# The order of four matmuls in the 64-row slots of an attention-score loop

## The chip, the cores and the metric

The kernel runs on one core of a Trainium2 chip. The metric is device time in microseconds (us), the median of three runs. The engines are called PE (TensorE; PEld is its loading of weights), DVE (VectorE), ACT (ScalarE), POOL (GpSimd) and SP (which issues most DMAs).

## The reference, cut to what matters

Eight images of 128 channels and 36x36 pixels go through a convolutional attention block, then each image's 1296 pixels become tokens of 128 features, then an additive attention over the tokens, then a mixture of experts. The additive attention is where the time goes, and the change touches nothing else:

```
def _L1_attn_ref(x, mask, Wq, bq, Wk, bk, w, bw):
    q = jnp.einsum('bld,ed->ble', x, Wq) + bq
    k = jnp.einsum('bld,ed->ble', x, Wk) + bk
    t = jnp.tanh(q[:, :, None, :] + k[:, None, :, :])
    scores = jnp.einsum('bijd,d->bij', t, w) + bw[0]
    attn = jax.nn.softmax(scores, axis=-1)
    return jnp.einsum('bij,bjd->bid', attn, x)
```

Every pair of tokens i, j needs a sum of 128 weighted tanh values. The kernel doesn't take the tanh of each pair. It groups five or six features, and writes the sum of their weighted tanh as one fraction: the denominator is a product of (exponential of the query + exponential of the key) terms, multiplied out into 32 (for five features) or 64 (for six) products of a query factor and a key factor, and the numerator has the same products with other weights. So a group's denominator and numerator are matmuls with a contraction of 32 or 64 rows.

## The kernel before, in words

**Units and slots.** The score loop runs over 264 units: 8 images x 3 chunks of 432 queries x 11 tiles of keys. Ten tiles of a chunk have 128 keys, one (the remainder) has 16. A unit of 128 keys has 12 slots, `k` = 0 to 11, in four triples. In a triple the first two slots (`k % 3` = 0 and 1) hold groups of five features: two matmuls with contractions of 32 rows each. The third (`k % 3` = 2) is a **slot of six**: its two halves are rows 0 to 63 and rows 64 to 127, and each half has its own PSUM bank. There are 4 x 240 = 960 slots of six. A remainder unit has two slots of its own form, made at line 1159.

**A slot's work.** `denominators(p + LAG)`, with `LAG` = 3, issues the two denominator matmuls of the slot three places ahead into one `d` tile of two banks (there are two such tiles, so the tile is free when ACT has read the slot two places before), and then ACT's logarithm over both banks (line 1177). An exponential follows on ACT (line 1180): for `k % 3` = 0 at once, for the two slots that follow together, after the second one's logarithm. That gives `lq`, one over the denominator. Then `numerators(p)` issues the two numerator matmuls of this slot into two of four `n` banks; `terms(p, ns)` has DVE multiply each by `lq` (line 1211 for most slots, where the results `rp` are added up by POOL at line 1220; lines 1200 to 1207 for `k` = 1, 4, 7 and 10, where DVE adds them up itself). All other work that needs a PSUM bank (convolutions, projections, transposes: the matmuls at lines 279 and 283) takes its banks from the same four, in turn.

**What sets the order.** The program is emitted by hand, and each engine runs its own instructions in that order, with semaphores between engines. `matmul_turn` puts the other work's matmuls behind the slots of six (`TURNS` = 2, 5, 8, 11). So within a slot of six PE has, in order: denominator half 0 and half 1 of the slot three ahead, numerator half 0 and half 1 of this slot, then other work if any is due. They will be called d0, d1, n0 and n1. `products` issues them (line 1154); each is float32 and leaves two load-and-multiply passes in the trace, so a slot leaves four passes named `d` and four named `n`.

For a slot of six `p` the slot `p + 3` is a slot of six too, except for the last slot before each of the 24 remainder units and for the end of the loop: 935 of 960.

Of the kernel before, what the change touches and what calls it, by code (L numbers as in the profile page):

```python
# [9 lines left out]
F32 = mybir.dt.float32  # L10
# [9 lines left out]
CH = 432  # L20
# [6 lines left out]
NKT = len(KT)  # L27
# [20 lines left out]
SLOTS = []  # L48
# [7 lines left out]
LAG = 3  # L56
# [15 lines left out]
def kernel(  # L72
# [29 lines left out]
    mm = nc.tensor.matmul  # L102
# [27 lines left out]
    with ExitStack() as loop, ExitStack() as score:  # L130

        def pool(name, bufs, stack=loop, side="left", space=bass.MemoryType.SB):
            return stack.enter_context(
                tc.tile_pool(name=name, bufs=bufs, side=side, space=space)
            )
# [13 lines left out]
        ps_d = pool("ps_d", 2, score, "right", bass.MemoryType.PSUM)  # L149

        ps_n = pool("ps_n", 4, space=bass.MemoryType.PSUM)
# [19 lines left out]
        def load_raw_taps(w, name):  # L171
# [36 lines left out]
            out=gavg3, in_=gavg3, compare_op=ALU.is_ge, fill=0.0, base=0,  # L208
# [3 lines left out]
            out=gavg3, in_=gavg3, compare_op=ALU.is_ge, fill=0.0, base=C // G - 1,  # L212
# [191 lines left out]
        def conv_keys(b):  # L404
            k = convolved["k"] = big_tile("k0")
            if b == 0:
                taps["k"] = load_taps("wk_t")
            for r0, nr in KROWS:
                yield from conv_turns(
                    taps["k"], (r0, nr), 1, grid(k[:, r0 * WV : (r0 + nr) * WV], WV), True  # L410
                )
# [471 lines left out]
        def gating(b):  # L883
            yield from gate_logits(b, range(NCH))
            yield from gate_tokens(b)
# [184 lines left out]
        def early_shares():  # L1070

            t = one.tile(list(xpad.shape), F32, tag="xpad", name="shares0").rearrange(
                "p a b -> p (a b)"
            )[:, :N]
            nc.sync.dma_start(t, gpair[0])
            shares_of[0] = [t[:, c * CH : (c + 1) * CH] for c in range(NCH)]
            shares_of[1] = load_pieces(
                gpair[1],
                lambda: kstp.tile([128, NF // 2, 128], F32, tag="ks", name="shares1").rearrange(
                    "p q t -> p (q t)"  # L1080
                )[:, :CH],
            )

        def first_weights():

            t = one.tile(list(xwin.shape), F32, tag="xwin", name="w0").rearrange(
                "p j n -> p (j n)"
            )
            w1s[0] = t[:, : EG * HID].rearrange("p (e h) -> p e h", e=EG)
            nc.sync.dma_start(w1s[0], weight1[:EG, :128, :].rearrange("e d h -> d e h"))  # L1090
            b1_s = t[:E, EG * HID : (EG + 1) * HID]
            nc.sync.dma_start(b1_s, weight1[:, 128, :])
            b2_s = t[:, (EG + 1) * HID : (EG + 1) * HID + O]
            for h in range(2):
                nc.sync.dma_start(b2_s[E * h : E * (h + 1)], weight2[:, HID, :])
            ffn_bias.extend((b1_s, b2_s))

        def residuals(n):

            for b in range(n):  # L1100
                load_residual(b)
                yield step()
# [10 lines left out]
        units = [(b, c, j) for b in range(NB) for c in range(NCH) for j in order]  # L1113
        slots = []
        for u, (b, c, j) in enumerate(units):
            slots += [(u, k) for k in range(len(REM_SLOTS) if j == NKT - 1 else NP)]
        kf_of, qf_of, lq_of, live = {}, {}, {}, {}

        def banks(u, k):
            return 2 if units[u][2] < NKT - 1 else len(REM_SLOTS[k])  # L1120
# [10 lines left out]
        def prefetch(u):  # L1131
            if u < len(units) and u not in kf_of:
                b, c, j = units[u]
                assert (b, j) in made
                n = 128 if j < NKT - 1 else 32
                kf = kfp.tile([128, NF, 128], F32, tag="kf", name="kf")
                nc.sync.dma_start(
                    kf[:, :, :n], kd[b][j].rearrange("p (q t) -> p q t", t=128)[:, :, :n]
                )
                kf_of[u] = kf  # L1140

        def new_block(b, c, q):
            qf = qfp.tile([128, 2, CH], F32, tag="qf", name="qf")
            qf_of[b, c, q] = qf
            return query_block(b, c, q, qf)

        def products(u, k, part, outs):

            b, c, j = units[u]
            kf = kf_of[u]  # L1150
            if j < NKT - 1:
                q, rows = SLOTS[k]
                for h in range(2):
                    mm(outs[h][:, :CH], kf[rows[h], q, :], qf_of[b, c, q][rows[h], part, :],  # L1154
                       start=True, stop=True)
                return
            for out, bank in zip(outs, REM_SLOTS[k]):
                for i, (q, rows) in enumerate(bank):
                    mm(out[32 * i : 32 * i + 32, :CH], kf[rows, q, :32],  # L1159
                       qf_of[b, c, q][rows, part, :], start=True, stop=True)  # L1160

        def denominators(p):

            if p >= len(slots):
                return
            u, k = slots[p]
            d = ps_d.tile([128, 2, 512], F32, tag="d", name="d")
            n = banks(u, k)
            products(u, k, 0, [d[:, h, :] for h in range(n)])
            g, o = group_of[p]  # L1170
            if g == p:
                alone = p in ends
                lq_of[g] = lp.tile(
                    [128, 2 if alone else 4, CH], F32, tag="lq1" if alone else "lq", name="lq"
                )
            lq = lq_of[g]
            nc.scalar.activation(lq[:, o : o + n, :], d[:, :n, :CH], AF.Ln)  # L1177
            if p in ends:
                some = lq[:, : o + n, :]
                nc.scalar.activation(some, some, AF.Exp, scale=-1.0)  # L1180

        def numerators(p):
            ns = [ps_n.tile([128, 512], F32, tag="n", name="n") for _ in range(banks(*slots[p]))]
            products(*slots[p], 1, ns)
            return [ps[:, :CH] for ps in ns]

# [37 lines left out]
        def sums(u):  # L1224

            s = live.pop("p")
            ending(u).tensor_add(s[:, 0, :], s[:, 0, :], s[:, 1, :])  # L1227
            d = live.pop("d")
            ending(u).tensor_add(d, s[:, 0, :], d)  # L1229
            return d  # L1230
# [49 lines left out]
        def take_turns(p, k):  # L1280
            for lane in lanes:
                if lane.due(p, False) and (k not in DVE_PAIRS or lane is first_of_all):
                    lane.run(p)
# [53 lines left out]
        for p in range(LAG):  # L1337
            denominators(p)
# [5 lines left out]
        for p, (u, k) in enumerate(slots):  # L1344
            b, c, j = units[u]
            rem = j == NKT - 1
            if k == 0:
                prefetch(u + 2)
                if c == 0 and j == 1:
                    if b > 0:  # L1350
                        gates.append(gating(b - 1))
                    if b == NB - 1:
                        gates.append(residuals(4))
                        first_weights()
                        early_shares()
                    if b + 1 < NB:
                        background.extend(
                            (normal(b + 1), conv_keys(b + 1), layer0(b + 1), tokens(b + 1),
                             keys(b + 1, range(NKT)))
                        )  # L1360
            take_turns(p, k)
            denominators(p + LAG)
            ns = numerators(p)
            terms(p, ns)
            if pending and pending[0][0] <= p:
                exps(p, *pending.popleft()[1:])
            last = p + 1 == len(slots) or slots[p + 1][0] != u

            if j == order[-1] and u + 1 < len(units):
                for q in NEXT_AT.get(k, ()):  # L1370
                    first_of_all.append(new_block(*units[u + 1][:2], q))
            elif j == order[-2] and last and u + 2 < len(units):
                first_of_all.append(new_block(*units[u + 2][:2], IN_TURN[0]))
            behind_rem = k == 0 and u > 0 and units[u - 1][2] == NKT - 1
            matmul_turn(
                p, k == 1 if rem else k in TURNS or behind_rem,
                lanes[:1] if behind_rem else lanes,
            )
            if last and rem:
                first_of_all.append(rem_scores(p, u, live.pop("rem")))  # L1380
            elif last:
                pending.append((p + 7, u, sums(u)))
# [74 lines left out]
    hidden, hidden_t, outs = {}, {}, deque()  # L1457
# [154 lines left out]
```

## Time and profile before

| | |
|---|---|
| median of 3 runs | 6008.39 us (6008.08 to 6008.49) |
| the profiled execution | 6001.25 us, of which the span of the trace is 5999.3 us |
| granted TensorE clock | 0.996 of full speed |
| score loop, 260 to 5880 us of the span: PE busy | 5304 of 5620 us |
| the same: ACT busy | 5189 us |
| the same: DVE busy | 4575 us |
| the same: POOL busy | 4396 us |
| denominators' and numerators' passes (line 1154) | 11,520 each, median 522 ns |

Matmul passes overlap: a pass of 432 columns is listed with 522 ns, but passes on the same rows begin 361 ns apart, and passes on different rows run beside each other. So PE's busy share says little by itself; the times at which passes begin say more.

### The profile page before, as it was taken

The page shows a single profiled execution, that of the slowest core. Times are in us where ns is not written, and L with a number is a line of the kernel's source. Part 1 is how long each engine was busy: PE and PEld are TensorE (multiplying, and loading weights), DVE is VectorE, ACT ScalarE, POOL GpSimd, SP SyncE. Part 2 cuts the span into 40 slices and gives each one's busy share as a digit, 9 for nine tenths or more (in the row PEclk, how much of TensorE's full clock was granted, in tenths as well). Part 3 has the DMA queues.
Part 4 walks back from the last instruction along what each step waited for, and adds up shares of the span by engine and source line. Part 5 has one row for each costly group of instructions (what it writes and reads, how often), then busy time and mean ns, then how long its engine had stood idle before and what let it go on. Part 6 is the DMA issues. An engine that isn't in the chain of part 4 may idle for free.

```text
span 5999.3 us, 94469 instructions
## 1 busy us (share of the span) xinstructions
PE 5629.9 (94%) x33507; PEld 2937.7 (49%) x33507; DVE 4780.5 (80%) x9566; ACT 5359.6 (89%) x5995; POOL 4581.9 (76%) x2870
## 2 busy tenths in 40 slices
PE   8999999999999999999999999999999999998888
PEld 5554455545554454544545445454445544544334
DVE  4787878878788788877888778887878878788884
ACT  3999999999989899889998989989998999999993
POOL 5777777877778868778788777877777777778872
PEclk9999999999999999999999999999999999999999
DMA  1200021001110011100111001110011100210007
GB/s 60 70 23 23 29 73 40 21 25 41 62 39 21 27 54 48 38 24 23 64 38 40 23 23 67 38 36 23 25 66 37 36 23 25 77 57 22 30 26 284
DMA packets 151705, 270.43 MB, mean 45 GB/s; under 512 B 45568, under 2 KB 77568, under 8 KB 151232
## 3 DMA queue, kind: packets, MB, share of 16 engines
q1 hardware_dynamic: 151008, 263.84, 13.0%
q8 instruction: 264, 4.33, 0.3%
q14 instruction: 209, 1.71, 0.1%
q10 hardware_dynamic: 224, 0.55, 0.0%
HBM read 200.15 MB, written 63.93 MB: 44 GB/s over the span
## 4 chain that ended last, share of the span: by engine, by line
PE 58%; DVE 23%; ACT 9%; issue 7%; POOL 2%; DMA 1%; DVEq 0%; POOLq 0%; ACTq 0%
PE d L1154 19%; PE n L1154 12%; DVE rp L1211 9%; PE pa L279 7%; DVE n L1205 7%; ACT lq L1177 6%; PE pc L279 5%; DVE accd L1207 4%; PE s L279 3%; PE pk L279 3%; PE pq L279 2%; PE n L1159 1%; PE d L1159 1%; POOL accp L1220 1%; ACT lq L1180 1%
## 5 line engine op out<-in xcount | busy, mean ns | idle before, releaser
L1220 POOL TENSOR_TENSOR accp<-accp,rp 128x864 f32<-128x864 f32 x1439 | 2911.2, 2023 | 962.1 <-DVE rp L1211 933.8
L1154 PE MATMUL n<-qf,kf 32*128 32x432 f32 (+1 forms) x11520 | 2996.2, 552 | 12.1 <-ACT qf L806 7.4
L1154 PE MATMUL d<-qf,kf 32*128 32x432 f32 (+1 forms) x11520 | 2777.2, 558 | 206.5 <-ACT lq L1177 197.6
L1177 ACT ACTIVATE lq<-d 128x864 f32<-128x864 f32 x2928 | 2480.1, 876 | 338.7 <-PE n L1154 252.7
L1211 DVE TENSOR_TENSOR rp<-n,lq 128x432 f32<-128x432 f32 x3912 | 2180.1, 600 | 701.0 <-PE n L1154 570.4
L1180 ACT ACTIVATE lq<-lq 128x864 f32<-128x864 f32 (+1 forms) x1944 | 2495.9, 1284 | 61.6
L1154 PEld LDWEIGHTS d<-qf,kf 32*128 32x128 f32 (+1 forms) x11520 | 1029.1, 184 | 1359.6 <-ACT lq L1177 997.1
L1154 PEld LDWEIGHTS n<-qf,kf 32*128 32x128 f32 (+1 forms) x11520 | 1259.9, 185 | 667.0 <-issue 286.8
L1207 DVE TENSOR_TENSOR accd<-n,accd 128x432 f32<-128x432 f32 x1440 | 866.1, 601 | 24.6
L1205 DVE TENSOR_TENSOR n<-n,lq 128x432 f32<-128x432 f32 x1440 | 809.4, 607 | 47.2 <-PE n L1154 29.0
L1218 POOL TENSOR_TENSOR accp<-rp 128x864 f32<-128x864 f32 x240 | 485.2, 2022 | 250.8 <-DVE rp L1211 250.0
L1229 POOL TENSOR_TENSOR accd<-accp,accd 128x432 f32<-128x432 f32 x239 | 265.0, 1109 | 18.7
L279 PE MATMUL pa<-xh,e 128*108 128x129 f32 x1920 | 251.0, 280 | 30.0 <-DVE accd L1207 28.7
L279 PEld LDWEIGHTS pa<-xh,e 128*108 128x108 f32 x1920 | 220.2, 173 | 118.3 <-DVE accd L1207 97.4
L1227 POOL TENSOR_TENSOR accp<-accp 128x432 f32<-128x432 f32 x239 | 263.7, 1103 | 12.2
L807 POOL TENSOR_SCALAR qf<-qf,cs_s 128x432 f32<-128x432 f32 x192 | 260.1, 1364 | 4.1 <-ACT qf L806 4.0
L477 POOL TENSOR_TENSOR tot<-tot,e 116x432 f32<-116x432 f32 x192 | 211.7, 1103 | 16.6 <-ACT e L486 13.2
L279 PE MATMUL s<-q,k 128*116 128x432 f32 x480 | 209.6, 548 | 9.5 <-DVE accd L1207 7.5
L279 PE MATMUL pa<-e,vw 116*128 116x432 f32 x480 | 200.8, 541 | 0.0
L279 PEld LDWEIGHTS pk<-xT,a_k 128*128 128x128 f32 x1408 | 165.6, 193 | 57.9 <-DVE accd L1207 42.8
L486 ACT ACTIVATE e<-s 116x432 f32<-116x432 f32 x240 | 118.8, 521 | 83.5 <-PE s L279 80.8
L279 PE MATMUL pk<-xT,a_k 128*128 128x128 f32 (+1 forms) x1408 | 180.7, 281 | 2.4 <-DVE accd L1207 1.3
(260 smaller groups left out, 3754.6 us busy)
## 6 DMA issues: line engine op xcount, KB each, us to landing
kf<-kd SPq DMA_DIRECT2D x239, 512.0 KB
kd<-ks SPq DMA_DIRECT2D x158, 256.0 KB
w<-in_weight_dram SPq DMA_DIRECT2D x32, 1024.0 KB
wk_t<-wk_t_d SPq DMA_DIRECT2D x7, 768.0 KB
wv_t<-wv_t_d SPq DMA_DIRECT2D x7, 768.0 KB
wq_t<-wq_t_d SPq DMA_DIRECT2D x7, 768.0 KB
x<-in_x_dram SPq DMA_DIRECT2D x8, 648.0 KB
t<-tokd SPq DMA_DIRECT2D x96, 54.0 KB
```

What stands on the lines that cost most here:

```text
L279: mm(out, lhsT, rhs, **kw)
L807: nc.gpsimd.tensor_scalar(qf[:, 1, :], qf[:, 0, :], feat["cs_s"][:, q : q + 1], None, ALU.mult)
L1154: mm(outs[h][:, :CH], kf[rows[h], q, :], qf_of[b, c, q][rows[h], part, :], start=True, stop=True)
L1177: nc.scalar.activation(lq[:, o : o + n, :], d[:, :n, :CH], AF.Ln)
L1180: nc.scalar.activation(some, some, AF.Exp, scale=-1.0)
L1205: mult(ns[h], ns[h], lq[:, o + h, :])
L1207: nc.vector.tensor_add(live["d"], ns[h], live["d"])
L1211: mult(rp[:, h, :], n, lq[:, o + h, :])
L1218: nc.gpsimd.tensor_add(live["p"], live["r"], rp)
L1220: ending(u if k == NP - 1 else 0).tensor_add(live["p"], live["p"], rp)
L1227: ending(u).tensor_add(s[:, 0, :], s[:, 0, :], s[:, 1, :])
L1229: ending(u).tensor_add(d, s[:, 0, :], d)
```

## The change

Where both slot `p` and slot `p + 3` are slots of six, the four matmuls are issued in the order n0, d1, d0, n1 in place of d0, d1, n0, n1. ACT's logarithm (and, where it is due, exponential) is emitted behind all four. The tiles, the number of instructions, their operands and their engines stay as they are; everywhere else the order stays too.

```diff
+        def is_six(p):
+            return p < len(slots) and units[slots[p][0]][2] < NKT - 1 and slots[p][1] % 3 == 2
...
+        def sixes(p):
+
+            outs = n_banks(p), d_banks(p + LAG)
+            for at, part, h in ((p, 1, 0), (p + LAG, 0, 1), (p + LAG, 0, 0), (p, 1, 1)):
+                u, k = slots[at]
+                q, rows = SLOTS[k]
+                out = outs[0][h] if part else outs[1][:, h, :]
+                mm(out[:, :CH], kf_of[u][rows[h], q, :], qf_of[(*units[u][:2], q)][rows[h], part, :],
+                   start=True, stop=True)
+            reciprocals(p + LAG, outs[1])
+            return [ps[:, :CH] for ps in outs[0]]
...
-            denominators(p + LAG)
-            ns = numerators(p)
+            if is_six(p) and is_six(p + LAG):
+                ns = sixes(p)
+            else:
+                denominators(p + LAG)
+                ns = numerators(p)
```

`d_banks` and `n_banks` allocate the tiles as `denominators` and `numerators` did, and `reciprocals(p, d)` is the second half of the old `denominators`: the logarithm and the exponential on ACT, unchanged.

More of the change, by code (lines that the diff above doesn't have):

```diff
@@ L1160, in products, with d_banks, n_banks @@
                        qf_of[b, c, q][rows, part, :], start=True, stop=True)
+        def is_six(p):
+            return p < len(slots) and units[slots[p][0]][2] < NKT - 1 and slots[p][1] % 3 == 2
+        def d_banks(p):
+            return ps_d.tile([128, 2, 512], F32, tag="d", name="d")
+        def n_banks(p):
+            return [ps_n.tile([128, 512], F32, tag="n", name="n") for _ in range(banks(*slots[p]))]
+        def sixes(p):
[8 more added lines that the diff above has]
+            return [ps[:, :CH] for ps in outs[0]]
         def denominators(p):
@@ L1165, in denominators, with reciprocals @@
                 return
[L1166 to L1169, printed above, removed]
+            d = d_banks(p)
+            products(*slots[p], 0, [d[:, h, :] for h in range(banks(*slots[p]))])
+            reciprocals(p, d)
+        def reciprocals(p, d):
+            n = banks(*slots[p])
             g, o = group_of[p]
@@ L1182, in numerators @@
         def numerators(p):
-            ns = [ps_n.tile([128, 512], F32, tag="n", name="n") for _ in range(banks(*slots[p]))]
+            ns = n_banks(p)
             products(*slots[p], 1, ns)
```

## The prediction

> **What bounds the kernel now.** I read the page's busy times first, then the list of waits, then the timeline around slots of six. The page (engine, busy us, share, instructions; then a group with its mean duration in ns and the idle time before it):
>
> ```profile
> PE 5629.9 (94%) x33507; PEld 2937.7 (49%) x33507; DVE 4780.5 (80%) x9566; ACT 5359.6 (89%) x5995; POOL 4581.9 (76%) x2870
> ...
> L1177 ACT ACTIVATE lq<-d 128x864 f32<-128x864 f32 x2928 | 2480.1, 876 | 338.7 <-PE n L1154 252.7
> ```
>
> Two engines share the bound: PE and ACT. Who waits for whom (us in total, times, longest):
>
> ```profile
> PEld d L1154 <- ACT lq L1177: 997.1, 1244, 2.7
> ...
> DVE rp L1211 <- PE n L1154: 570.4, 661, 10.5
> ...
> ACT lq L1177 <- PE n L1154: 252.7, 312, 2.9
> ...
> PE d L1154 <- ACT lq L1177: 197.6, 395, 2.0
> ```
>
> PE waits for ACT to free a d tile (197.6 us of true idleness), and ACT waits for PE's denominators (252.7 us, put down to the n passes that end beside them). Neither has much to spare. The timeline shows a stretch without other work (start, duration, engine, operation, count, idle before):
>
> ```profile
> 3000.13 0.87 ACT L1177 ACTIVATE lq<-d 128x864 f32<-128x864 f32 x1
> ...
> 3001.06 0.99 PE L1154 MATMUL d<-qf,kf 64*128 64x432 f32 x4 [0.84 <-ACT lq L1177]
> ...
> 3001.86 1.66 ACT L1177 ACTIVATE lq<-d 128x864 f32<-128x864 f32 x2
> 3001.89 0.89 PE L1154 MATMUL n<-qf,kf 64*128 64x432 f32 x4
> ...
> 3002.79 0.63 PE L1154 MATMUL d<-qf,kf 32*128 32x432 f32 x2
> ...
> 3002.88 1.12 DVE L1211 TENSOR_TENSOR rp<-n,lq 128x432 f32<-128x432 f32 x2 [0.85 <-PE n L1154]
> ```
>
> Here ACT bounds: the logarithm ends at 3001.00, d0 and d1 begin at 3001.06 after 0.84 us of idle PE. n0 and n1 begin 0.83 us later, the next slot 0.90 us after that. d is complete at 2.05 (that is, 3002.05); the second logarithm of the "x2", the one that reads it, begins at 1.86 + 1.66 - 0.89 = 2.63. So it has 0.58 us to spare. And a stretch with other work:
>
> ```profile
> 5290.47 0.99 PE L1154 MATMUL d<-qf,kf 64*128 64x432 f32 x4
> ...
> 5291.05 1.65 ACT L1177 ACTIVATE lq<-d 128x864 f32<-128x864 f32 x2
> ...
> 5291.30 0.89 PE L1154 MATMUL n<-qf,kf 64*128 64x432 f32 x4
> ...
> 5292.73 1.64 ACT L1180 ACTIVATE lq<-lq 128x1728 f32<-128x1728 f32 x1
> ...
> 5294.28 0.87 ACT L1177 ACTIVATE lq<-d 128x864 f32<-128x864 f32 x1
> ...
> 5295.21 0.99 PE L1154 MATMUL d<-qf,kf 64*128 64x432 f32 x4 [0.24 <-ACT lq L1177]
> ```
>
> Here PE came to the slot late: no idle time before d. ACT's logarithms, exponential and next logarithm follow without a gap, and the next slot of six waits for the last of them.
>
> I measured all 935 slots from the trace's single passes in this way. In **463 PE came late** (no idle before d beyond the 0.09 us of changing from 32 to 64 rows); in the other 472 it had waited, 225.6 us in all.
>
> **The change, part by part.** Nothing is removed: four matmuls on two row halves before, four after.
>
> *PE's own time.* Before, d0 beside d1, then n0 beside n1: 0.83 + 0.90 us. After, where nothing waits, n0 beside d1, then d0 beside n1: the same. Where PE waits for ACT, n0 now runs in the wait; but rows 64 to 127 still have d1 and then n1 to do from the logarithm's end, the same 1.7 us, and the next slot, of 32 rows, begins only when n1 has ended (2.79 against 1.89 + 0.89 = 2.78 above). So the filled wait is worth **0**.
>
> *The logarithm, where PE came late (463).* d0 is now in the second pair, so d is complete where n was: 0.83 + 0.89 = 1.72 after the slot's start, against 0.99, some 0.72 us later. The spare time of the logarithm there is 0.43 us in the mean (median 0.41). Late logarithms, slot by slot, max(0, 0.72 + wait for n0 - spare): 167 us in 381 slots. In the 5290 stretch: d complete at 1.46 becomes 2.18, the logarithm moves from 1.81 to 2.2, nearly 0.4 us. What ACT then loses it can regain in its own later gaps before the next slot of six. At 2414.02 the first logarithm of a triple begins after 0.25 us of idleness, which would swallow most of it; at 5294.28 there is none. Subtracting those gaps slot by slot leaves 87 us. The rest is swallowed where the next slot's d tile had been free for a while when PE arrived; subtracting that too leaves **42 us**. At 5295.21 PE was waiting already, so there the whole 0.3 to 0.4 us count.
>
> *The logarithm, where PE had waited (472).* n0 begins in the wait, so d0 is held back by 0.43 us in the mean, and the logarithm can spare 0.54 or more: 17 us late, 6 after ACT's gaps, **1 us** at the end.
>
> *The wait of n0.* n0's bank is freed by DVE's product of the slot two before. At the old place of n0 it was free in nearly all slots. At the new place, 0.83 us earlier, it isn't in 83 of the 463, by 15 us together. Behind it in PE's queue stand d1 and d0, for whose bank ACT is long done. Does a waiting n0 hold them up? The row: in the stretch above an n pass on other rows begins at 3003.62, ahead of d passes (3003.63) that were issued before it, so passes of different rows don't keep strict order once issued. The Trainium skill's "TensorE: Matmul & The Clock Gate", Part 3, under what overlaps and what doesn't, says that matmuls start and end strictly in program order, and only weight loads are pulled ahead. By a free order this costs 0, by the rule **15 us** on PE. The rule speaks against the change, and since the row's 0.01 us are of passes past their waits, I take the rule. In the waiting slots n0 is often some 0.1 us late, in front of an idle PE: 5 us at most, taken as **5**.
>
> *DVE.* It can multiply n0 up to 0.7 us earlier, n1 as before; the second product then ends up to 0.55 us sooner, where DVE stood idle (0.85 us in the stretch above). Such waits before a six's first product, cut at 0.57 us each, sum to 72 us, but only 25 us of them lie in front of a next slot to which PE comes late; before the others ACT is what PE waits for. In most slots to which PE comes late DVE has a backlog and doesn't wait for n0. Ends: 0 and -25; I take **-8**, since few of these products are the ones that PE waits for.
>
> POOL's sum needs both products; it has 76% of the span and its waits are not on PE's path: 0. No DMA moves. In the end: 42 + 1 + 15 + 5 - 8 = **+55 us**. Against the profiled execution's 6001.25 that is 6056; the median of the runs stands 7.1 us above it, so 6063.
>
> **The rivals.**
> 1. *ACT's slack is worth less than I count.* A late logarithm uses up gaps that an earlier one counted already, and the leeway of the next slot goes too. Without the leeway of the next slot's d tile: 87 + 6 + 20 = +113, that is 6121; with nothing absorbed at all, 167 + 17 + 20 = +204, that is 6212, an extreme. For it: ACT has 92% of the loop. Against it: its 430 us of gaps lie mostly before the first logarithm of a triple, just behind the six.
> 2. *DVE is the loop's true pace-maker*, and n0 in front pays: the chain of waits has DVE at 23%, through products of n. If all 72 us came through and a late logarithm were absorbed (it needs a mean absorption of 0.36 us in 381 slots), the time would be 6008 - 72 + 20 = 5956; with the 25 us that lie before late slots and nothing else, 5983. It decides once the earlier second product brings more than the 55 + 8 us of cost, about 0.07 us in each of 935 slots. Against it: DVE waited for n before only some 250 of them.
> 3. *No difference*: ACT's gaps swallow all of the delay, and PE's lateness at n0 is recovered while it would have waited for DVE in the next slots of five: within 12 us of 6008.
>
> That the order does not come out as written is unlikely: each engine keeps the emitted order.
>
> **How the numbers follow.** A kernel of 6008 us can be told from itself within about 0.2%, 12 us; that is what "same" means here. My forecast's case (+20 to +90): 0.52; rival 1: 0.24; rival 3: 0.12; rival 2: 0.12. Some of the forecast's case ends in "same": faster 0.12, same 0.12, slower 0.76. The likeliest case has 6028 to 6098 for itself. The range reaches up into rival 1 and down over rival 3, 6003 to 6130.
>
> **What would show it.** Right: the logarithm's idle time (338.7 us, 252.7 of it from PE) grows by over 50 us, and now in front of a six's logarithm too; in late slots the d passes of a six end 0.7 us later; PE's idle time before d doesn't fall in sum, and the passes of a slot of six still take 1.7 us where nothing waits; DVE's 570.4 us of waiting for n falls. Wrong: ACT's idle time unchanged or smaller, or slots of five (whose n passes now start up to 0.5 us late) becoming shorter by more than ACT loses.

## The result, and the profile after

| | before | changed |
|---|---|---|
| median | 6008.28 us (5 runs, 6006.62 to 6008.49) | 6059.85 us (5 runs, 6055.9 to 6061.79) |
| ratio, with 95% interval | | 1.0084 (1.0073 to 1.0096) |
| profiled execution, span | 6001.25, 5999.3 us | 6058.24, 6056.3 us |

The change costs 52 us. Forecast were 6063 us, in a range of 6003 to 6130. What was line 1177 before is line 1201 now, 1211 is 1235, and the four matmuls of the 935 reordered slots are line 1178. First the page of the changed kernel (busy us, share, instructions; then groups with busy us, mean ns, and the idle time before them):

```profile
PE 5797.1 (96%) x33507; PEld 3074.5 (51%) x33507; DVE 4774.7 (79%) x9566; ACT 5394.2 (89%) x5995; POOL 4584.9 (76%) x2870
...
L1201 ACT ACTIVATE lq<-d 128x864 f32<-128x864 f32 x2928 | 2521.8, 878 | 380.0 <-PE n L1154 202.8
L1235 DVE TENSOR_TENSOR rp<-n,lq 128x432 f32<-128x432 f32 x3912 | 2185.7, 599 | 712.9 <-PE n L1154 498.9
...
L1178 PE MATMUL d<-qf,kf 64*128 64x432 f32 x3740 | 1429.6, 553 | 45.4 <-ACT lq L1201 45.0
```

PE is busier by 167 us with the same 33,507 passes: a wait for ACT in which an n0 now runs is counted as busy. That is no gain. ACT has 34.6 us more of busy time and 22.4 us more of idle time (span less busy: 639.7 before, 662.1 now), together the 57.0 us by which the span grew. The idle time before its logarithms went from 338.7 to 380.0. The list of waits says where the new part is (us in total, times, longest):

```profile
PEld n L1178 <- DVE rp L1235: 592.8, 839, 1.8
...
ACT lq L1201 <- PE n L1154: 202.8, 264, 2.9
PEld d L1178 <- ACT lq L1201: 146.2, 170, 1.7
...
ACT lq L1201 <- PE n L1178: 97.2, 300, 1.4
```

The first line is idle time of the weight loads alone, with passes mostly still running beside it; PE itself stood idle before an n0 for want of DVE for 15.2 us by the page. The last line is new: 300 times ACT stood in front of a six's logarithm for a pass of line 1178 that ends the slot. It is put down to n1, which ends beside d0. Counted over the single logarithms of the two traces: the gaps before those of slots of six grew from 40.8 us (49 gaps) to 136.0 us (349), those before the first logarithm of a triple shrank from 262.4 to 211.5 us. This is the timeline of PE in a slot to which PE came late (start, duration, engine, operation, count):

```profile
3028.89 0.63 PE L1178 MATMUL n<-qf,kf 64*128 64x432 f32 x1
3028.90 0.63 PE L1178 MATMUL d<-qf,kf 64*128 64x432 f32 x1
3029.36 0.52 PE L1178 MATMUL n<-qf,kf 64*128 64x432 f32 x1
3029.37 0.88 PE L1178 MATMUL d<-qf,kf 64*128 64x432 f32 x2
3029.73 0.52 PE L1178 MATMUL n<-qf,kf 64*128 64x432 f32 x1
3030.09 0.52 PE L1178 MATMUL d<-qf,kf 64*128 64x432 f32 x1
3030.09 0.52 PE L1178 MATMUL n<-qf,kf 64*128 64x432 f32 x1
3030.54 0.63 PE L1154 MATMUL d<-qf,kf 32*128 32x432 f32 x2
```

n0 and d1 run beside each other, then d0 and n1. The last d pass ends at 3030.61, 1.72 us after the slot's start, where it was 0.99 before. ACT in the same stretch:

```profile
3029.57 0.87 ACT L1201 ACTIVATE lq<-d 128x864 f32<-128x864 f32 x1
3030.64 0.89 ACT L1201 ACTIVATE lq<-d 128x864 f32<-128x864 f32 x1 [0.21 <-PE n L1178]
3031.57 1.64 ACT L1204 ACTIVATE lq<-lq 128x1728 f32<-128x1728 f32 x1
3033.12 0.87 ACT L1201 ACTIVATE lq<-d 128x864 f32<-128x864 f32 x1
```

The logarithm begins 0.03 us after that pass has ended, with 0.21 us of idle time in front, and the exponential and the next logarithm follow late without a gap that could make up for it. The next slot of six pays:

```profile
3032.76 0.99 PE L1178 MATMUL n<-qf,kf 64*128 64x432 f32 x2
3034.04 0.99 PE L1178 MATMUL d<-qf,kf 64*128 64x432 f32 x4 [0.29 <-ACT lq L1201]
3034.87 0.88 PE L1178 MATMUL n<-qf,kf 64*128 64x432 f32 x2
3035.78 0.63 PE L1154 MATMUL d<-qf,kf 32*128 32x432 f32 x2
```

Here n0 runs in PE's wait for that logarithm, as the change has it. But d1 and n1 are still to come on rows 64 to 127, and the next slot begins 3035.78 - 3034.04 = 1.74 us after d; before it was 1.73 (3001.06 to 3002.79). The wait is filled and nothing is saved.

### The profile page after: what moved, and what is told of

Read it like the earlier page. It is cut to its first block, busy times and chain, and to the rows that moved or that the text cites. A ratio compares the mean times of both kernels' runs of the same rounds, so it can differ in the third digit from the quotient of the medians.

```text
span 6056.3 us, 94481 instructions
## 1 busy us (share of the span) xinstructions
PE 5797.1 (96%) x33507; PEld 3074.5 (51%) x33507; DVE 4774.7 (79%) x9566; ACT 5394.2 (89%) x5995; POOL 4584.9 (76%) x2870
## 4 chain that ended last, share of the span: by engine, by line
PE 63%; DVE 21%; ACT 7%; issue 7%; POOL 1%; DMA 1%; DVEq 0%; POOLq 0%; ACTq 0%
PE d L1154 14%; PE n L1154 9%; PE n L1178 8%; DVE rp L1235 8%; PE pa L279 7%; DVE n L1229 7%; PE d L1178 6%; PE pc L279 5%; ACT lq L1201 5%; DVE accd L1231 3%; PE s L279 3%; PE pk L279 3%; PE pq L279 2%; PE n L1159 1%; PE d L1159 1%
## 5 line engine op out<-in xcount | busy, mean ns | idle before, releaser
L1201 ACT ACTIVATE lq<-d 128x864 f32<-128x864 f32 x2928 | 2521.8, 878 | 380.0 <-PE n L1154 202.8
L1235 DVE TENSOR_TENSOR rp<-n,lq 128x432 f32<-128x432 f32 x3912 | 2185.7, 599 | 712.9 <-PE n L1154 498.9
L1154 PE MATMUL n<-qf,kf 32*128 32x432 f32 x7780 | 2121.8, 564 | 21.0 <-ACT qf L806 12.4
L1154 PE MATMUL d<-qf,kf 32*128 32x432 f32 (+1 forms) x7780 | 1832.3, 550 | 17.9 <-ACT lq L1201 15.6
L1178 PE MATMUL n<-qf,kf 64*128 64x432 f32 x3740 | 1685.3, 549 | 42.2 <-DVE rp L1235 15.2
L1178 PE MATMUL d<-qf,kf 64*128 64x432 f32 x3740 | 1429.6, 553 | 45.4 <-ACT lq L1201 45.0
L1154 PEld LDWEIGHTS n<-qf,kf 32*128 32x128 f32 x7780 | 851.3, 183 | 371.2 <-ACT qf L806 74.1
L1154 PEld LDWEIGHTS d<-qf,kf 32*128 32x128 f32 (+1 forms) x7780 | 732.1, 184 | 569.8 <-ACT lq L1201 263.1
L1178 PEld LDWEIGHTS n<-qf,kf 64*128 64x128 f32 x3740 | 624.2, 186 | 717.2 <-DVE rp L1235 592.8
L1178 PEld LDWEIGHTS d<-qf,kf 64*128 64x128 f32 x3740 | 562.6, 186 | 310.4 <-ACT lq L1201 146.2
L1251 POOL TENSOR_TENSOR accp<-accp 128x432 f32<-128x432 f32 x239 | 263.8, 1104 | 12.2
```

The costliest lines, as they stand in the source:

```text
L1178: mm(out[:, :CH], kf_of[u][rows[h], q, :], qf_of[(*units[u][:2], q)][rows[h], part, :], start=True, stop=True)
L1235: mult(rp[:, h, :], n, lq[:, o + h, :])
```

## The experiments

Two theories stood against each other. **L**: what costs is that d is complete 0.72 us later, so that ACT's logarithm is late. **W**: what costs is that n0, in front, may wait for its bank and holds d up.

**d1 in front.** No numerator stands ahead of d1 any more, and d is as late as in the change.

```diff
-            for at, part, h in ((p, 1, 0), (p + LAG, 0, 1), (p + LAG, 0, 0), (p, 1, 1)):
+            for at, part, h in ((p + LAG, 0, 1), (p, 1, 0), (p + LAG, 0, 0), (p, 1, 1)):
```

> Order d1, n0, d0, n1 in the same 935 slots: nothing stands in front of d any more, and d is still complete only with the second pair. Theory L (the cost is the late logarithm): in the slots to which PE comes late nothing changes against the changed kernel, and in the 472 slots in which PE waits for ACT n0 can no longer use the wait, so d is 0.72 us late there too against 0.54 us to spare: some 50 to 85 us more on ACT. About 6115 us (6085 to 6150), slower than the changed kernel's 6060. Theory W (the cost is that n0's wait for its bank holds d up): the wait is gone, about 6008 us.

Measured: 6086.84 us (6086.26 to 6088.31), ratio to before 1.013 (1.0114 to 1.0145). The timeline of one of its slots, first PE, then ACT:

```profile
2042.76 0.63 PE L1178 MATMUL d<-qf,kf 64*128 64x432 f32 x1 [0.36 <-ACT lq L1201]
```

```profile
2043.57 1.84 ACT L1201 ACTIVATE lq<-d 128x864 f32<-128x864 f32 x2
```

PE had waited for ACT here. Two logarithms in a row took 1.65 us before; the second now begins 0.19 us late for want of d, as 0.72 less the spare 0.54 would have it. Of the sixes' logarithms 703 now have a gap in front, against 349 in the changed kernel. The wait isn't gone, as the expectation had it, since n0 still stands ahead of d0: in 113 slots n0 began later than d1, by 16.1 us together, about as much as it holds up in the changed kernel (15.8 us, see under n1 in front). But with no more of that wait the cost is larger: W alone falls. L had the direction, but the cost over the changed kernel is 27 us, not 50 to 85, at the low end of the range that was expected.

**d0 ahead of d1.** The same passes on each row half, in another order of issue.

```diff
-            for at, part, h in ((p, 1, 0), (p + LAG, 0, 1), (p + LAG, 0, 0), (p, 1, 1)):
+            for at, part, h in ((p, 1, 0), (p + LAG, 0, 0), (p + LAG, 0, 1), (p, 1, 1)):
```

> Order n0, d0, d1, n1: each row half has the same passes in the same order as in the changed kernel; only the issue order between the halves differs. If passes on different rows run freely of one another once issued: the same as the changed kernel, about 6060 us. If passes start strictly in the order of the program, d1 starts only with d0, n0 and n1 run alone, and each of the 463 late slots takes up to 0.72 us more of PE: 6200 to 6390 us.

Measured: 6062.05 us (6061.59 to 6064.56), the changed kernel's time. Its timeline of PE:

```profile
3001.78 0.63 PE L1178 MATMUL n<-qf,kf 64*128 64x432 f32 x1
3001.79 0.63 PE L1178 MATMUL d<-qf,kf 64*128 64x432 f32 x1
3002.24 0.52 PE L1178 MATMUL n<-qf,kf 64*128 64x432 f32 x1
3002.26 0.87 PE L1178 MATMUL d<-qf,kf 64*128 64x432 f32 x2
3002.62 0.52 PE L1178 MATMUL n<-qf,kf 64*128 64x432 f32 x1
```

The d pass at 3001.79 can only be d1, since d0's rows have n0 on them. It starts beside n0, ahead of d0, which was issued before it (d0's first pass is the later one of the "x2", which starts at 3002.26 + 0.87 - 0.52 = 3002.61). In 421 of the 935 slots d1 starts beside n0 in this way. Passes whose waits are over start free of each other on different row halves.

That raises a question for L: the semaphore that tells ACT of a finished d is on the last pass issued, here d1's, and in 767 slots this pass ended over 0.3 us before d0's. Had ACT gone on it, d would have been early again. It didn't: no logarithm of the 935 began before d0's last pass had ended, and in 322 of the 767 slots ACT stood idle until just after it (0.05 to 0.06 us). The starts are free, but the end is reported in the order of issue, so that d was as late here as in the changed kernel.

**n1 in front.** This was meant to make the wait in front longer: n1's bank was taken to come free one product of DVE later than n0's.

```diff
-            for at, part, h in ((p, 1, 0), (p + LAG, 0, 1), (p + LAG, 0, 0), (p, 1, 1)):
+            for at, part, h in ((p, 1, 1), (p + LAG, 0, 0), (p + LAG, 0, 1), (p, 1, 0)):
```

> Order n1, d0, d1, n0: the mirror image, except that the bank of n1 comes free one DVE product (0.55 us) later than that of n0. Read from the trace of before, n1 would not be ready when PE arrives in 296 late slots (89 us together), and in the waiting slots it would outlast PE's idle time by 117 us. Theory W (a numerator in front that waits holds d up): 150 to 250 us slower than the changed kernel, about 6250 us. If a waiting numerator holds nothing up: about 6060 us, like the changed kernel.

Measured: 6066.4 us (6063.6 to 6068.01), 4 us above the variant before it, which ran on the same chip. The 206 us of waits that I had counted didn't come, and the reason is in the trace. One of its slots, DVE and then PE:

```profile
407.25 1.12 DVE L1235 TENSOR_TENSOR rp<-n,lq 128x432 f32<-128x432 f32 x2
```

```profile
407.91 0.63 PE L1178 MATMUL n<-qf,kf 64*128 64x432 f32 x1
```

The two products of the slot two before run until 408.37, yet n1 begins at 407.91, 0.05 us after the first of them. So it is in 673 of the 935 slots: the numerator in front begins before the second product has ended, and never earlier than 0.05 us after the first. The banks are given out in the order in which they are used, and n1 in front gets the one that n0 had. The wait in front was therefore not made longer. I counted it in both traces as the time by which a slot begins later than both PE and its d tile are ready: 15.9 us in 95 slots here, 15.8 us in 95 in the changed kernel. So this variant doesn't test W. It leaves n0 for last instead, and DVE waits 81.6 us before `rp` for passes of line 1178, against 5.2 in the changed kernel; whether the 4 us come from that is not shown.

**ACT relieved**, in the kernel before and in the changed one:

```diff
-                some = lq[:, : o + n, :]
+                some = lq[:, : o + n, : CH // 2]
...
-            nc.scalar.activation(e[:, : d.shape[-1]], d, AF.Exp, bias=feat["eb_s"])
+            nc.scalar.activation(e[:, : d.shape[-1]], d, AF.Exp, bias=feat["eb_s"], scale=0.0)
```

> The kernel before with ACT relieved: the exponential of line 1180 covers half of the columns (some 1200 us of ACT less), and the last exponential of the scores is taken of zero times the score. Leaves out half of the reciprocals, so the scores are not used. PE and DVE bound then; some 100 to 300 us faster than 6008. Serves as the base of the next one.

> The changed kernel with ACT relieved in the same way. Theory L (late logarithm): ACT has room for 0.72 us of delay, so the difference to the relieved kernel before shrinks from 52 us to at most 20. Theory W (n0 in front holds d up): PE comes late to every slot then, and the difference stays at 50 us or grows.

Measured: 5892.67 us (5892.22 to 5896.86) and 5892.73 us (5888.97 to 5894.02); the ratios to the kernel before, 0.9813 (0.9799 to 0.9828) and 0.9811 (0.9796 to 0.9825), can't be told apart. From the page of the relieved kernel before:

```profile
L1177 ACT ACTIVATE lq<-d 128x864 f32<-128x864 f32 x2928 | 2508.8, 879 | 1069.1 <-PE n L1154 770.7
```

and of the relieved changed one:

```profile
L1201 ACT ACTIVATE lq<-d 128x864 f32<-128x864 f32 x2928 | 2560.8, 879 | 1113.6 <-PE n L1154 567.6
```

ACT has over 1000 us of gaps before its logarithms in both. The late d adds 44.5 us to them, as much as in the full kernels (41.3), and here they cost nothing. With ACT off the bound the loss is gone, although n0 stands in front of d as before and holds slots up for 30.5 us by the count above. Together with the variant with d1 in front, in which the wait was the same and the cost larger, this decides for L. The granted clock differs a little between the two (0.985 to 0.988, and 0.988 to 0.991), but at 0.988 in both, 5892.57 us stand against 5893.43 and 5894.02. Nor does the change gain anything here, where PE is busy for 95% of the span.

**DVE relieved**, again in both:

```diff
-                    for h in range(2):
-                        nc.vector.tensor_add(live["d"], ns[h], live["d"])
```

> The kernel before with DVE relieved: the 1440 additions of line 1207 (867 us of DVE) are left out, so three of four products of these slots are missing from the scores. Banks come free sooner. ACT bounds: some 20 to 150 us faster than 6008. Serves as the base of the next one.

> The changed kernel with DVE relieved in the same way. Theory L: ACT is as full as before, the difference to the relieved kernel before stays at 30 us or more. Theory W: n0's bank is nearly always free when PE comes, the difference falls to 10 us or less.

Measured: 5911.31 us (5909.86 to 5913.14) and 5964.07 us (5959.84 to 5966.36), 52.8 us apart. From the pages of the two, before and changed:

```profile
L1177 ACT ACTIVATE lq<-d 128x864 f32<-128x864 f32 x2928 | 2475.5, 876 | 265.5 <-PE n L1154 201.0
```

```profile
L1201 ACT ACTIVATE lq<-d 128x864 f32<-128x864 f32 x2928 | 2514.4, 877 | 317.3 <-PE n L1154 167.2
```

With 15% less of DVE's work the cost is what it was, and so is what the late d adds to the gaps (51.8 us). That speaks for L, but less than was meant: n0's wait went only from 15.8 to 10.9 us, in 75 slots, so W was not switched off.

**One slot of each unit.** In `if is_six(p) and is_six(p + LAG):` a condition `k == 8` or `k == 11` was added.

> The new order only in the slots k = 8 (239 of the 935), in whose triple ACT also takes a unit's last exponential ahead of the logarithm, so that the logarithm has 1.1 us to spare instead of 0.4 to 0.6. Theory L: 9% of the late logarithms counted in the trace of before lie here (16 of 184 us), so 4 to 8 us of the changed kernel's 52: 6012 to 6016 us. A flat cost of each reordered slot: 26%, 13 us or more: 6021 us.

> The new order only in the slots k = 11 (215 of the 935). Theory L: 33% of the late logarithms (61 of 184 us), so 17 us: 6023 to 6028 us, three times the cost of k = 8 alone. A flat cost of each slot: 23%, 12 us: 6020 us, no more than k = 8 alone.

Measured: 6016.28 us, ratio 1.0014 (1.0006 to 1.0023), and 6018.72 us, ratio 1.0019 (1.0013 to 1.0026). In us that is 4 to 14, and 8 to 16. The first is at the upper edge of what L had expected (6012 to 6016), the second below it (6023 to 6028) and near the flat cost's 6020: the times don't separate a cost in proportion to the late logarithms from a flat one. The gaps before the sixes' logarithms do differ as counted: 40.8 us before, 48.8 with k = 8, 81.9 with k = 11. But with k = 11 the gaps before the next first logarithms fell by 24 us and gave more than half of it back. How the loss is shared among the four slots stays open.

**Other work elsewhere**, in the kernel before:

```diff
-                p, k == 1 if rem else k in TURNS or behind_rem,
+                p, k == 1 if rem else k % 3 == 0 or behind_rem,
```

> The kernel before, with the other work's matmuls behind the slots k = 0, 3, 6 and 9 instead of behind the slots of six. Theory L says that what counts is how late a logarithm's d comes against the time it has to spare: behind a slot of six the next d has 1.3 us to spare in the stretch without other work, behind a slot with k % 3 = 0 it has 2.2 us. If that is what ACT's 262 us of idle time before these logarithms come from, 0 to 60 us faster than 6008; if the other engines' order matters more, slower.

Measured: 6208.92 us, ratio 1.0333 (1.0319 to 1.0347). From its page:

```profile
L1177 ACT ACTIVATE lq<-d 128x864 f32<-128x864 f32 x2928 | 2534.0, 879 | 492.7 <-PE n L1154 371.2
```

The gaps before the first logarithms all but went, from 262 to 14 us, but 380 us stand before the second ones instead (23 before), and the logarithms' idle time is 154 us larger in all. The expectation (up to 60 us faster, if L's spare time was all) is missed. The spare time that I had read from a stretch without other work doesn't hold where there is some. None of the experiments led to a version that beats the kernel before.

## Why the prediction was right, point by point

*PE's own time, 0.* Right, and seen in the slot at 3034.04: 1.74 us against 1.73. In the 90 slots in which d waited and a slot of five follows directly, it is 1.73 us in the median. The idle time ahead of the slots of six fell from 226 to 72 us, but 255 us lie now between a slot's start and its first d, with n0 inside: d itself waits no less.

*The late logarithm, 42 + 1 us.* The mechanism is shown by the relieved pair and by d1 in front. The 0.72 us is right (1.72 against 0.99). The idle time before the logarithms grew by 41.3 us, where I had said "over 50" in what would show it. But that is not the whole loss. ACT's busy time grew by 34.6 us: a logarithm begins some 0.09 us before the instruction ahead of it ends (1.65 us for two of 0.88), and one that comes late loses that overlap. Summed over all neighbours on ACT, overlaps fell from 322.6 to 293.2 us; the other 5.2 us are slightly longer durations (876 and 878 ns for a logarithm). The other way, idle time before the rest of ACT's work fell by 18.9 us, mostly before the tiles `hpre` (12.2) and `ri` (4.9), which are other work. 41.3 + 34.6 - 18.9 = 57.0 us, the growth of the span. The sum had neither of the last two.

*The wait of n0, 15 + 5 us.* The wait was counted rightly: 15.8 us in 95 slots, against 15 in 83. What it costs is not shown. A held slot makes d late, so it is no term beside the logarithms' idle time but one of its causes, and it is too small to be the main one. Of the rule that I took for it, from the Trainium skill's page "TensorE: Matmul & The Clock Gate", Part 3, on what overlaps and what doesn't: that matmuls start strictly in program order isn't so between the row halves here (3001.79 above). What the term needed does hold: an instruction with an open wait holds up what is issued behind it. In the kernel before, n0's bank was free and PE ready ahead of d in 456 of the 472 slots in which PE waited for a d tile, for 182 us together, and n0 never began before d.

*DVE, -8 us.* DVE's waits before a six's first product did fall, from 76 to 1 us, about the 72 us that I had put down. They brought nothing: before the first product of the slots with `k % 3` = 0, which follow, the waits grew from 566 to 647 us. For all idle time before `rp`, this is the line of before, to be held against the 712.9 of line 1235 above:

```profile
L1211 DVE TENSOR_TENSOR rp<-n,lq 128x432 f32<-128x432 f32 x3912 | 2180.1, 600 | 701.0 <-PE n L1154 570.4
```

So the mechanism is right, and that the sum of +55 us comes so near is in part luck: 15 + 5 - 8 = +12 us for n0 and DVE stand where the runs show +34.6 - 18.9 = +15.7 us of something else.

*Rival 1*, that more of the lateness comes through (+113), is out by size; *rival 2*, DVE as pace-maker, by the pair with DVE relieved, which differs by 52.8 us as before; *rival 3*, no difference, holds only once ACT has room. Two slips in the working changed nothing: rival 2's 167 us in 381 slots are 0.44 us each, not 0.36, and a case that begins at +20 us has no part in "same", which means 12 us.

## What to carry to other kernels

When two matmuls change places, ask for each of them who reads it and how long that reader could have waited. Here the one that came earlier fed an engine with time to spare, and the one that came later fed the engine that bounds. Filling an engine's wait with work saves time only if the end of the stretch moves too: look at the last instruction on the same rows, not at the idle time. To test such a reason, relieve the suspected engine in both kernels and see whether the difference goes; and look in the trace whether the wait in question became shorter or longer at all, which it hardly did in three of these experiments.

## What the runs showed of the hardware that was not expected

On ACT a gap costs more than its length: in the changed kernel busy time grew by 34.6 us with the same instructions, 29.4 of them from overlap that was lost, since a logarithm that follows directly begins some 0.09 us before the instruction ahead ends.

On PE, passes on rows 64 to 127 began ahead of passes on rows 0 to 63 that were issued earlier (3001.79 against 3002.61), so the issue order of two matmuls on different halves made no difference to the time: 6062.05 against 6059.85 us, in intervals that overlap (1.0071 to 1.0105 and 1.0073 to 1.0096). Two things did keep the order of issue: the semaphore of a pass that had ended over 0.3 us early let no logarithm begin before the pass issued ahead of it had ended (767 slots), and in the kernel before no n0 began ahead of a d that was waiting for its tile, though in 456 slots its bank was free and PE ready.
